# Inverse root of a recurrence's output norm: ScalarE logarithm and exponential in place of square root and VectorE reciprocal

## The chip, the cores and the metric

One core of a Trainium2 chip runs the whole program. The metric is the device time of one execution in microseconds (us). A core has five engines that run side by side, each through its own list of instructions, in the order of that list: TensorE (PE in the profile; its weight loads are PEld), VectorE (DVE), ScalarE (ACT), GpSimd (POOL) and SyncE (SP, which here only issues DMA transfers). They wait for one another by semaphores. ScalarE evaluates functions such as the square root from a table, and an instruction of its own (ACT_TABLE_LOAD in the profile) brings in another set of functions.

## The reference, cut to what matters

The reference runs two layers. Layer 0 is a recurrence over 32 mini-batches of 16 tokens for 4 sequences and 32 heads of 16 channels, beside a gated feed-forward layer; layer 1 is an attention with compressed keys and values beside an expert layer. All is float32. The change concerns the norm of the recurrence's output, which is taken over the 16 channels of each head:

```python
def _ln(x, gamma, beta):
    mu = x.mean(-1, keepdims=True)
    var = x.var(-1, keepdims=True)
    return gamma * ((x - mu) / jnp.sqrt(var + EPS)) + beta      # EPS = 1e-6, 16 channels
...
Z1_bar = xq @ W1_s - eta_mb * Attn1 @ grad + b1_bar
out = xq + _ln(Z1_bar, ln_w, ln_b)
...
out = ys.transpose(1, 0, 3, 2, 4).reshape(Bb, Ll, HS)
out = _ln(out, post_norm_weight, post_norm_bias)               # over 512 channels
return out @ o_w.T
```

## The kernel before, in words

**The first stage** (0 to about 1030 us) does layer 0. The 512 tokens of each sequence are cut into 8 chunks of 64; a chunk of all four sequences has 256 columns (CW), and four mini-batches. The outer loop runs over the 32 mini-batches. Each step (`weights_out`, `first_product`, `queries_out`, `gradient`, `out_operands`, `update`, `emit_out`) is a chain through all engines: products of the state with keys and queries into `pz` and `pso`, a norm and its gradient on VectorE with small ScalarE operations (L339 to L373), block-diagonal copies `g_bd` on VectorE and ScalarE (L378), `gh` on GpSimd (L404), the update of the state `wacc` on PE, and copies of the new state into `wq_bd` (L315) and `wh` (L318) for the next step.

**Filling work.** Between the parts of a step, `fill(us)` takes pieces of other work from a generator and gives PE something to do: `between(ch)` holds, for each chunk, the feed-forward layer (`gate_up`: 11 pairs of gate and up products `pf` into two PSUM buffers, a Silu `sg` on ScalarE, L458, and a product `hid` on VectorE, L459; `down`: products `pd`), the features of the next chunk (`norm_turn` transposes the normed input into `xT`, copied by ScalarE, L140; `keys`, `queries`, `token_tile`) and `finish(ch - 1)`, the norms of the chunk that the recurrence has just left. Each piece names a number of microseconds as its share. No chunk's steps begin before its features are done. `finish` is called 8 times, once for each chunk; I number the calls by it. Its first part is put after the ninth of the 11 gate pairs. For chunk 6 the pieces come at other places, and for chunk 7, where no feed-forward work is left, `finish` runs between the `latents` products. From all this the builder makes one list for each engine, and within the program's dependences it puts instructions of different pieces in another order than they are written.

**`finish(ch)`** works on `zb`, the chunk's centred output, 128 partitions by 4 blocks of 256 columns. ScalarE squares it (L524). Then twice, for two blocks at a time (128x512): PE sums each group of 16 partitions by a product with `bones` (L528, into a `pj` PSUM buffer, of which there are two for all uses); ScalarE takes the root of the mean plus epsilon into `rs` (named `pn_rs`, one buffer for both halves, L530); VectorE inverts it (L531) and multiplies `zb` by it (L532). ScalarE applies weight and bias in four operations (L534), GpSimd adds the queries (L537). The second norm follows: VectorE adds the four blocks up (L516, L517), PE multiplies by `onesd` for the mean (L540, `pj<-pn_sq,onesd` in the profile), VectorE subtracts it (L541), ScalarE squares (L542), VectorE adds up, PE sums (L548), ScalarE takes a root of 128x2 (L549), and PE multiplies by `wo` (L554). PE products go through the helper at L100, so they carry its line and are told apart by their tiles.

**The later stages** (from 1030 us) do the expert layer and the attention, and are bound by PE; nothing in them is touched.

Of the kernel before, what the change touches and what calls it, by code (L numbers as in the profile page):

```python
# [13 lines left out]
AF = mybir.ActivationFunctionType  # L14
# [9 lines left out]
NH, HD, K = 32, 16, 16  # L24
# [31 lines left out]
def trunk_kernel(ctx: ExitStack, tc: tile.TileContext, a: dict, out: bass.AP):  # L56
    nc = tc.nc
# [17 lines left out]
    eps_ttt = const.tile([P, 1], F32, tag="eps_ttt", name="eps_ttt")  # L75
# [13 lines left out]
    with ExitStack() as px:  # L89
# [9 lines left out]
        def mm(out, lhsT, rhs, start=True, stop=True):  # L99
            nc.tensor.matmul(out, lhsT=lhsT, rhs=rhs, start=start, stop=stop, skip_group_check=True)  # L100

        def psum():
            return ps_pj.tile([P, 512], F32, tag="pj", name="pj")
# [10 lines left out]
        def row_norm(dst, src, nm):  # L114
            st = wk.tile([P, 6], F32, tag="ln_st", name=f"ln_st{nm}")
            mv = wk.tile([P, 2], F32, tag="ln_mv", name=f"ln_mv{nm}")
            nc.vector.bn_stats(out=st, in_=src)
            nc.vector.bn_aggr(out=mv, in_=st)
            rs = wk.tile([P, 1], F32, tag="ln_rs", name=f"ln_rs{nm}")
            nc.scalar.activation(rs, mv[:, 1:2], AF.Sqrt, bias=eps_ln, scale=1.0)  # L120
            nc.vector.reciprocal(rs, rs)
            nc.vector.tensor_scalar(dst, src, mv[:, 0:1], rs, ALU.subtract, ALU.mult)

        def transposed(src):
            pt = psum().rearrange("p (c t) -> p c t", c=NC)
            for c in range(NC):
                nc.tensor.transpose(pt[:, c, :], src[:, c * P : (c + 1) * P], ident)
            return pt
# [385 lines left out]
        def over_blocks(t, z):  # L514

            nc.vector.tensor_add(t[:, :2], z[:, :2], z[:, 2:])  # L516
            nc.vector.tensor_add(t[:, 0], t[:, 0], t[:, 1])  # L517
            return t[:, 0]

        def finish(ch):  # L520
            store = nc.sync if ch + 1 < NCHUNK else nc.scalar
            zb = zbs.pop(ch)
            sq = wk.tile([P, NC, CW], F32, tag="pn_sq", name=f"pn_sq_{ch}", bufs=1)
            nc.scalar.activation(sq, zb, AF.Square)  # L524
            for j in range(2):
                half = zb[:, 2 * j : 2 * j + 2].rearrange("p c t -> p (c t)")
                pv = psum()
                mm(pv, bones, sq[:, 2 * j : 2 * j + 2].rearrange("p c t -> p (c t)"))  # L528
                rs = wk.tile([P, 512], F32, tag="pn_rs", name=f"pn_rs_{ch}_{j}", bufs=1)
                nc.scalar.activation(rs, pv, AF.Sqrt, bias=eps_ttt, scale=1.0 / HD)  # L530
                nc.vector.reciprocal(rs, rs)  # L531
                nc.vector.tensor_mul(half, half, rs)  # L532
            for be in range(NC):
                nc.scalar.activation(  # L534
                    zb[:, be], zb[:, be], AF.Identity, bias=beta_ch[:, be : be + 1], scale=gamma_ch[:, be : be + 1]
                )
            nc.gpsimd.tensor_add(zb, zb, q1[ch])  # L537
            yield 1.72
            pm = psum()[:, :CW]
            mm(pm, onesd, over_blocks(sq, zb))  # L540
            nc.vector.tensor_sub(zb, zb, pm.unsqueeze(1).to_broadcast([P, NC, CW]))  # L541
            nc.scalar.activation(sq, zb, AF.Square)  # L542
            over_blocks(sq, sq)
            yield 0.43
            pt = psum()
            rt = wk.tile([P, 2], F32, tag="pn_rt", name=f"pn_rt_{ch}")
            for u in range(2):
                mm(pt[:, u : u + 1], sq[:, 0, u * P : (u + 1) * P], onesd[:, :1])  # L548
            nc.scalar.activation(rt, pt[:, :2], AF.Sqrt, bias=eps_ttt, scale=1.0)  # L549
            nc.vector.reciprocal(rt, rt)  # L550
            for u in range(2):
                po = psum()
                for be in range(NC):
                    mm(po, zb[:, be, u * P : (u + 1) * P], wo[:, be, :], be == 0, be == NC - 1)  # L554
                t = yf.pop((ch, u))
                nc.vector.scalar_tensor_tensor(t, po, rt[:, u : u + 1], t, ALU.mult, ALU.add)
                for b2 in range(2):
                    store.dma_start(
                        out=yd[2 * u + b2, ch * CT : (ch + 1) * CT, :], in_=t[b2 * CT : (b2 + 1) * CT, :]
                    )  # L560

                xt = wk.tile([P, HS], F32, tag="xt", name=f"x1_{ch}_{u}", bufs=4)
                row_norm(xt, t, f"1_{ch}_{u}")
                xns[ch, u] = xt
                yield 4.4
            if ch >= NCHUNK - 2:
                t = wk.tile([P, NC, CW], F32, tag="xT", name=f"xl_{ch}", bufs=3)
                part = parts[ch] = t.rearrange("p c w -> p (c w)").rearrange("p (u c e x) -> p u c e x", u=2, c=NC, e=E)
            for u in range(2):
                if ch >= NCHUNK - 2:  # L570
                    xs = part[:, u]
                else:
                    xs = wk.tile([P, NC, E, 32], F32, tag="xs", name=f"xs_{ch}_{u}")
                nc.scalar.copy(xs, transposed(xns.pop((ch, u))).rearrange("p c (j e) -> p c e j", e=E))
                store.dma_start(out=xe_d[2 * ch + u], in_=xs)
                yield 0.6
# [50 lines left out]
        def between(ch):  # L627

            fin = finish(ch - 1) if ch > 0 else iter(())
            if ch + 1 == NCHUNK:  # L630
                latent_operands()
# [120 lines left out]
        for n in range(NM):  # L752
# [12 lines left out]
            if n + 1 < NM:  # L765
                while (n + 1) // CH not in done:
                    fill(1.0)
                pre = prepare(n + 1)
        fin = finish(NCHUNK - 1)
        for us in LAST_FINISH:  # L770
            fill(us)
# [15 lines left out]
    scale = 1.0 / math.sqrt(D)  # L787
# [493 lines left out]
```

## Time and profile before

| | us |
|---|---|
| median of three runs | 2126.29 (2125.87 to 2128.31) |
| the profiled execution | 2126.91 |
| its span, first to last instruction | 2125.1 |
| PE busy | 2041.5 |
| DVE busy | 1199.9 |
| ACT busy | 860.5 |
| POOL busy | 504.4 |
| all ACT_TABLE_LOAD instructions, 87 | 111.6 |
| granted PE clock, mean | 0.988 of full speed |

The 111.6 us are 87 times 1283 ns. A line of the profile that names a group gives line, engine, operation, output and inputs with their shapes, the count, then busy time in us and the mean ns of one, then the idle time of the engine just before them and what ended it. A line of the waits gives who waited for whom, the total, the number of times and the longest. A line of the timeline gives start, duration, engine, line, operation and count, and in brackets the idle time before it. PE's busy time is modelled, since matmuls overlap; a busy PE is one that has work, not one at its peak.

### The profile page before, as it was taken

What the parts mean: (1) busy time and instruction counts of PE and PEld (TensorE: products, weight loads), DVE (VectorE), ACT (ScalarE), POOL (GpSimd) and SP (SyncE); (2) the same over time, 40 slices, a digit from 0 to 9 for tenths busy, and PEclk for the clock granted to TensorE, in tenths of its full rate; (3) what the DMA queues carried; (4) which work ended last, traced back from release to release, by engine and by line L of the source; (5) the groups of instructions that cost most, each with busy time, mean ns of one, the idle gap of its engine ahead of it and who ended that gap; (6) DMA issues with size and microseconds to landing.
All of it is one profiled execution on the core that took longest, in us unless ns stands there. A gap on an engine that the chain in (4) does not pass through costs nothing.

```text
span 2125.1 us, 29355 instructions
## 1 busy us (share of the span) xinstructions
PE 2041.5 (96%) x9932; PEld 1169.6 (55%) x9932; DVE 1199.9 (56%) x2452; ACT 860.5 (40%) x1733; POOL 504.4 (24%) x555
## 2 busy tenths in 40 slices
PE   8999999999999998997899999999999999999999
PEld 6777777767676765744344344444444444444444
DVE  5445656565737475633111485766666665766663
ACT  2334343434334343312001364555545554555552
POOL 5233333323333332302000121111111111142110
PEclk9999999999999999999999999999999999999999
DMA  6546464645454646445831143443334333433332
GB/s 187 161 133 185 120 190 116 193 114 174 138 165 127 183 120 200 116 123 178 300 98 29 29 99 79 93 98 79 78 81 106 78 80 73 101 78 76 91 96 75
DMA packets 336496, 257.19 MB, mean 121 GB/s; under 512 B 107099, under 2 KB 264988, under 8 KB 335324
## 3 DMA queue, kind: packets, MB, share of 16 engines
q1 hardware_dynamic: 322320, 243.89, 42.8%
q10 hardware_dynamic: 11500, 5.32, 0.9%
q0 software_dynamic: 2528, 6.12, 0.8%
q8 instruction: 80, 1.31, 0.3%
q14 instruction: 68, 0.56, 0.1%
HBM read 159.50 MB, written 29.62 MB: 89 GB/s over the span
## 4 chain that ended last, share of the span: by engine, by line
PE 78%; DVE 6%; SPq 6%; DMA 4%; ACT 3%; issue 2%; POOL 1%; ACTq 0%; DVEq 0%; POOLq 0%
PE pj L100 14%; PE pf L100 11%; PE po L1119 9%; PE pc L1106 8%; PE sc L1038 8%; PE pq L1028 7%; PE pd L100 5%; SPq L1098 4%; PE epo L957 3%; PE epu L906 2%; PE pso L100 2%; PE pk L1020 2%; PE epg L906 2%; PE pz L100 2%; SPq L845 1%
## 5 line engine op out<-in xcount | busy, mean ns | idle before, releaser
L1013 POOL TENSOR_TENSOR kT<-t_k,t_k 32x512 f32<-32x512 f32 x64 | 80.7, 1260 | 802.6 <-PE pq L1028 339.9
L1043 ACT ACTIVATE prob<-sc,mx 128x512 f32<-128x512 f32 x256 | 174.3, 683 | 198.9 <-DVE mx L1040 194.1
L1038 PE MATMUL sc<-kT,qT 96*128 96x512 f32 x512 | 230.9, 593 | 1.7 <-ACT prob L1043 1.4
L1119 PE MATMUL po<-vo,ctxT 128*128 128x512 f32 x512 | 230.0, 592 | 0.7 <-ACT ctxT L1108 0.7
L1106 PE MATMUL pc<-prT,lv 128*128 128x512 f32 x496 | 224.8, 596 | 3.2 <-DVE t_q L1003 3.2
L1067 DVE STREAM_TRANSPOSE tt<-prob 128x512 f32<-128x512 f32 x252 | 173.0, 706 | 56.2 <-ACT prob L1048 48.5
L1028 PE MATMUL pq<-cq,uq 128*128 128x512 f32 x384 | 178.0, 600 | 7.3 <-ACT ctxT L1108 7.3
L100 PE MATMUL pf<-xT,wg 128*128 128x256 f32 x704 | 173.5, 389 | 8.2 <-DVE hid L459 7.1
L1048 ACT ACTIVATE prob<-prob,sm 128x512 f32<-128x512 f32 x256 | 176.4, 713 | 0.0
L1040 DVE TENSOR_REDUCE mx<-sc 128x1 f32<-128x512 f32 x256 | 168.2, 678 | 5.8 <-PE sc L1038 3.8
L100 PE MATMUL pf<-xT,wu 128*128 128x256 f32 x704 | 167.5, 381 | 0.0
L1038 PEld LDWEIGHTS sc<-kT,qT 96*128 96x128 f32 x512 | 96.9, 190 | 126.1 <-issue 120.1
L100 PE MATMUL pd<-wd,hid 128*128 128x512 f32 x352 | 164.7, 600 | 1.4 <-DMA wd<-in_wd 1.4
L1119 PEld LDWEIGHTS po<-vo,ctxT 128*128 128x128 f32 x512 | 96.9, 190 | 123.4 <-issue 117.9
L1106 PEld LDWEIGHTS pc<-prT,lv 128*128 128x128 f32 x496 | 94.7, 191 | 123.2 <-issue 118.4
L100 PEld LDWEIGHTS pf<-xT,wg 128*128 128x128 f32 x704 | 132.1, 192 | 34.9 <-DVE hid L459 10.1
L100 PEld LDWEIGHTS pf<-xT,wu 128*128 128x128 f32 x704 | 134.4, 191 | 18.9 <-DMA wu<-in_wu 0.4
L1028 PEld LDWEIGHTS pq<-cq,uq 128*128 128x128 f32 x384 | 73.6, 192 | 101.9 <-issue 90.5
L459 DVE SCALAR_TENSOR_TENSOR hid<-pf,us,sg 128x256 f32<-128x256 f32 x88 | 41.9, 478 | 139.1 <-ACT sg L458 138.4
L297 POOL TENSOR_SCALAR sk<-k,m 128x256 f32<-128x256 f32 x64 | 60.1, 950 | 182.4 <-PE pz L100 173.7
L1003 DVE SCALAR_TENSOR_TENSOR t_k<-pk,b_UK,trig_k 32x512 f32<-32x512 f32 x64 | 47.9, 748 | 90.4 <-ACT kT L1021 89.8
L100 PEld LDWEIGHTS pd<-wd,hid 128*128 128x128 f32 x352 | 63.8, 190 | 61.8 <-issue 48.6
(247 smaller groups left out, 3065.0 us busy)
## 6 DMA issues: line engine op xcount, KB each, us to landing
prT<-tt SPq DMA_DIRECT2D x1008, 64.0 KB, 2.0
wd<-in_wd SPq DMA_DIRECT2D x176, 256.0 KB, 3.0
wg<-in_wg SPq DMA_DIRECT2D x88, 256.0 KB, 2.9
wu<-in_wu SPq DMA_DIRECT2D x88, 256.0 KB, 3.4
rows<-rows SPq DMA_DIRECT2D x128, 66.0 KB, 2.2
kv<-rows SPq DMA_DIRECT2D x32, 264.0 KB, 4.5
gu<-in_gu SPq DMA_DIRECT2D x3, 2048.0 KB, 7.8
xt<-in_x SPq DMA_DIRECT2D x32, 128.0 KB, 3.3
```

Source lines behind the costliest of these rows:

```text
L100: nc.tensor.matmul(out, lhsT=lhsT, rhs=rhs, start=start, stop=stop, skip_group_check=True)
L906: nc.tensor.matmul(ps, lhsT=w[:, c, col : col + P], rhs=xe[:, :, c, e, :], start=(c == 0), stop=(c == NC - 1))
L1013: nc.gpsimd.tensor_sub(t[RD:mid, :], t1[RD:mid, :], t2[RD:mid, :])
L1028: nc.tensor.matmul(pq, lhsT=w[f"uq{i}"][:, h, :], rhs=cq[:, i, b, :], start=(i == 0), stop=(i == nq - 1))
L1038: pin(nc.tensor.matmul(ps, lhsT=qT[:KQ, i * P : (i + 1) * P], rhs=kT[:KQ, :], start=True, stop=True))
L1040: pin(nc.vector.tensor_reduce(mx, ps, AX.X, ALU.max, negate=True))
L1043: pin(nc.scalar.activation(pr, ps, AF.Exp, bias=mx, scale=1.0, accum_out=sm))
L1048: pin(nc.scalar.mul(pr, pr, sm))
L1067: nc.vector.transpose(out=tt[:, :, :, i, :], in_=pr.rearrange("p (kb e j) -> p kb e j", e=2, j=K))
L1098: nc.sync.dma_start(out=prT[32 * kq : 32 * kq + 32, :, qb, :], in_=src[32 * qb : 32 * qb + 32, :, kq, :])
L1106: pin(nc.tensor.matmul(pc, lhsT=lv[:, b, k, :], rhs=prT[:, k, :], start=(k == 0), stop=(k == E - 1)))
L1119: nc.tensor.matmul(po[e], lhsT=ctxT[:, h, e * P : (e + 1) * P], rhs=w["vo"][:, h, :], start=(h == 0), stop=(h == HPG - 1),)
```

## The change

In `finish`, the root by ScalarE and the inverse by VectorE become a logarithm and an exponential, both by ScalarE: 1/sqrt(v) = exp(-0.5 ln v). The product with `zb` stays, and so do all buffers. The other roots of the kernel (L120, L347, L549) keep their form. The lines behind the change move by one.

```diff
                 rs = wk.tile([P, 512], F32, tag="pn_rs", name=f"pn_rs_{ch}_{j}", bufs=1)
-                nc.scalar.activation(rs, pv, AF.Sqrt, bias=eps_ttt, scale=1.0 / HD)
-                nc.vector.reciprocal(rs, rs)
+
+                nc.scalar.activation(rs, pv, AF.Ln, bias=eps_ttt, scale=1.0 / HD)
+                nc.scalar.activation(rs, rs, AF.Exp, scale=-0.5)
                 nc.vector.tensor_mul(half, half, rs)
```

## The prediction

> **What bounds the kernel now.** I read the page's busy times first, then the two norm lines in the groups, then the waits of PE up to 1050 us (the recurrence lies there, the eight calls of `finish` between 187 and 985 us), and then the timeline of each call, because what counts is who waits at that place.
>
> ```profile
> PE 2041.5 (96%) x9932; PEld 1169.6 (55%) x9932; DVE 1199.9 (56%) x2452; ACT 860.5 (40%) x1733; POOL 504.4 (24%) x555
> ```
>
> PE is the bound, and every engine runs a list that was fixed at build time. So an instruction costs time only where it makes PE wait, and PE waits wherever its next instruction is not ready, even if later ones are. The groups that the change touches, with two neighbours that give prices:
>
> ```profile
> L1048 ACT ACTIVATE prob<-prob,sm 128x512 f32<-128x512 f32 x256 | 176.4, 713 | 0.0
> ...
> L530 ACT ACT_TABLE_LOAD x13 | 16.7, 1283 | 0.2
> ...
> L530 ACT ACTIVATE pn_rs<-pj,eps_ttt 128x512 f32<-128x512 f32 x16 | 11.0, 688 | 10.7 <-DVE zb L532 8.4 <-PE pj L100 2.2
> ```
>
> ```profile
> L531 DVE RECIPROCAL pn_rs<-pn_rs 128x512 f32<-128x512 f32 x16 | 53.6, 3350 | 19.8 <-ACT pn_rs L530 19.8
> ...
> L532 DVE TENSOR_TENSOR zb<-zb,pn_rs 128x512 f32<-128x512 f32 x16 | 11.0, 688 | 0.1
> ```
>
> The reciprocal is the longest single operation of VectorE here, and a ScalarE table load costs nearly two activations. Where PE waits:
>
> ```profile
> PE wacc L100 <- DVE g_bd L378: 11.5, 3, 9.3
> ...
> PE pj L100 <- DVE pn_sq L517: 3.3, 4, 1.7
> PE pso L100 <- POOL gh L404: 3.0, 3, 1.3
> ```
>
> The 9.3 us is one wait, in the call for chunk 6 (I write F0 to F7 for the eight calls). The 3.3 us are waits of the mean's product (L540) for the end of the norm chain (L517). In the windows around F0 to F7 (209 us together) PE is busy 186.9 us: **22 us** is all that the change could win back there. F6 in the timeline:
>
> ```profile
> 832.48 1.28 ACT L530 ACT_TABLE_LOAD   x1
> ...
> 833.77 0.69 ACT L530 ACTIVATE pn_rs<-pj,eps_ttt 128x512 f32<-128x512 f32 x1
> ...
> 834.49 3.35 DVE L531 RECIPROCAL pn_rs<-pn_rs 128x512 f32<-128x512 f32 x1 [2.46 <-ACT pn_rs L530]
> ...
> 839.38 3.35 DVE L531 RECIPROCAL pn_rs<-pn_rs 128x512 f32<-128x512 f32 x1 [0.81 <-ACT pn_rs L530]
> ...
> 844.90 2.50 POOL L537 TENSOR_TENSOR zb<-zb,q 128x1024 f32<-128x1024 f32 x1 [12.96 <-ACT zb L534]
> ...
> 850.71 1.08 PE L100 MATMUL wacc<-g_bd,km 128*32 128x64 f32 x32 [9.31 <-DVE g_bd L378]
> ```
>
> Both reciprocals stand ahead of the gradient's last operations in VectorE's list, so PE, which ran dry at 841.4, gets `g_bd` only at 850.7.
>
> **Counts.** Removed: 16 reciprocals, 53.6 us of VectorE. Sixteen square roots become sixteen Ln of the same operands (I take 0.69 us, the row's price). Added: 16 Exp from SBUF; the nearest rows are 0.68 (an Exp from PSUM, L1043) and 0.71 (a scaled copy from SBUF, L1048); I take 0.71, and an error of 0.1 us in all 32 would be 3 us at most. Table loads, counted in the built order of instructions: one stands before every Ln and every Exp (32, with two different set numbers, where the square roots had 13), the Silu line has 30 for 34, the second root 4 for 1: 105 for 87, or 18 x 1.283 = 23.1 us. ScalarE gets 23.1 + 11.4 = **34.5 us more**, and all of it in the eight places. Over 180 to 980 us ScalarE is busy 306 of 800 us, so the total has cover; the place decides.
>
> **The chain, alone.** From the first load to the data of the mean's product. Before: load 1.28, then twice (root 0.69, reciprocal 3.35, product 0.69), Identity x2 1.09, POOL addition 2.35, two additions 0.69 + 0.43 = **15.3 us**. After: load 1.28, Ln 0.69, load 1.28, Exp 0.71, product 0.69, and then, since there is one `pn_rs` buffer and the built order puts the next load behind the wait for that product, again load 1.28, Ln 0.69, Identity 0.54, load 1.28, Exp 0.71; in F0 to F3 and F5 an Identity 0.54, a Silu load 1.28 and a Silu 0.47 come ahead of the last two Identities (1.09), and the same 3.47 follow: **16.0 us**. Without the Silu (F6, F7; the product 0.69 counts instead) 14.4. So 53.6 us of reciprocals leave, and the chain of each call hardly changes: the loads take their place.
>
> **What moves.** The builder orders by its own estimate, and in the built order the mean's product comes sooner on PE: ahead of L540 there are 14.3, 17.8, 17.5, 17.5, 19.3 and 16.7 us of PE work after the group-sum products in F0 to F5 (before: 20.6, 21.2, 19.7, 21.4, 20.6, 19.9), and in F6 none at all (before: the whole of ten gate products). These are my sums of row prices (a gate pair 3.45, a 512-wide product 0.86, and so on). A chain no shorter, and a PE that comes for it sooner, is a wait.
>
> F6, walked with the rows: Ln done at 834.46, Exp 836.45, product 837.2, second Ln 839.2, Exp 841.75, product 842.5, Identities 843.4, POOL 845.8, additions 847.0. PE stands from 834.3 to 847.0 (12.7 us), then the mean's product, gate pairs 2 and 3 (6.9, and some 1.7 more, since the first group after the long wait now takes 3.57 instead of 1.89 us), and `wacc` at about 856; `g_bd` is ready by 853.6 then. Before, both pairs were done and `wacc` began at 850.7 after its wait; the next pair began at 853.0, now at 856.5, with the mean's product (0.5) already behind it: **+3.0**.
>
> The others the same way, by when PE has done an equal amount: F0 **+4.5** (the ScalarE copies of `wq_bd` and Silu 9, 10 queue behind the loads: `pz` waits 2.7 us, then the mean's product 2.4); F1 **+1.0** (1.6 us for the mean's product, partly given back); F2 **+3.5** (the chunk's transposed input, L140, and the mean's subtraction, L541, come late, and the next chunk's keys wait for both); F3 **+2.5** (the same two); F4 **-1.3** (the waits 1.6 for `g_bd` and 1.3 for `gh` shrink: VectorE is free earlier); F5 **+0.9** (1.6 for `wacc`, 2.1 for the mean); F7 **-1.0** (same PE order, latent products released a little earlier). Sum **+13.1**. Later waits of PE that hang on DMA (3.0 us of idle time in 480 to 500, 3.1 in 600 to 620) will swallow some; I take 2 off: **+11**. The profiled execution took 2126.9 (span 2125.1), the median of the three runs is 2126.3; from the median, **2137**.
>
> **A rule against the row.** In the rows above the load starts 0.02 us after the activation ahead of it (831.41 + 1.05) and the root 0.01 us after the load; all 87 loads take 1283 ns and no more. The Trainium skill ("ScalarE: Activation LUTs", section "What ACT_TABLE_LOAD costs") gives the same 1283 ns, and a drain of some 1380 ns beside it, 2.66 us for a switch. By that each call's chain would be about 5 x 1.38 = 6.9 us longer and the sum some 50 us higher, an estimate from that page which no gap in this trace supports. The same page (section "Table sets: the hidden batching unit") says that a logarithm and then an exponential need one load, from a set that holds both. That would take 2.6 us off each chain and turn the forecast to about no change; the built order has two, so I go by the order.
>
> **Rivals.** (a) *Faster, 2118.* VectorE's release decides: with 53.6 us gone there, the gradients come sooner, and of the 22 us of PE idle time some 8 go. For it: the 9.3 us wait, F4. Against: PE's list puts the mean's product ahead of `wacc` in F6. It decides once the chain is under some 13 us, that is if a load is hidden under the product or the additions. (b) *Same, 2126.* The added waits are swallowed downstream, since PE waits again on DMA (`kv`, `wd`) in every chunk and the recurrence's own chain is shorter without reciprocals. Against: after F0, F1, F4 such idle time is under 1.5 us per 20 us. (c) *Much slower, 2150.* The waits on PE also delay the recurrence step under way and drop the granted clock (0.74 in 840 to 860 after the 9.3 us wait), costing 1.7 us or more a call in addition: 13 + 8 x 1.4 = 24. (d) *One load serves each pair* though two are listed: 16 x 1.28 = 20 us less ScalarE work, 5 us of it on PE's waits: 2121.
>
> **Numbers.** Forecast 0.57, (a) 0.11, (b) 0.17, (c) 0.12, (d) 0.03. The ends without any cover are -22 and +34.5 us; the cases do not reach them. Leaving out (a) and the upper part of (c): **2121 to 2149**. A measurement of this kernel can tell about 0.2% (4.3 us) from no change: faster (a) and half of (d), 0.12; within, (b), the other half of (d) and the forecast's lower edge, 0.21; slower 0.67.
>
> **What would show it.** 32 loads on the two new lines at 1283 ns with nothing between load and activation; Ln and Exp near 0.69; the second Ln's load starting after the first product; in F6 a wait of PE for L517 near 12 us in place of 9.3 for `g_bd`; waits for L517 of 1 to 2.5 us in F0 to F5, and together some 20 us for the 3.3 now. I am wrong if PE finds the mean ready in F0 to F3, if F6's wait is under 9 us, or if the loads run while ScalarE waits.

## The result and the profile after

The changed kernel takes 2138.7 us (median of four runs, 2136.8 to 2141.1) where the kernel before, beside it, took 2126.1: a ratio of 1.0058, interval 1.0042 to 1.0074, or 12.6 us more. The forecast was 2137. A second comparison (experiment 5) gave 1.0069 [1.0051, 1.0087]. The profiled execution took 2141.1 us, its span was 2139.3.

The page of the changed kernel, busy times:

```profile
PE 2038.5 (95%) x9932; PEld 1168.9 (55%) x9932; DVE 1142.4 (53%) x2436; ACT 894.1 (42%) x1767; POOL 503.5 (24%) x555
```

VectorE lost 57.5 us, ScalarE gained 33.6, PE has the same work and stands 100.8 us (span less busy time) instead of 83.6. The groups of the changed lines (one line down from before):

```profile
L531 ACT ACT_TABLE_LOAD x16 | 20.5, 1283 | 4.2 <-DVE zb L533 4.0
L532 ACT ACT_TABLE_LOAD x16 | 20.5, 1283 | 0.3
...
L531 ACT ACTIVATE pn_rs<-pj,eps_ttt 128x512 f32<-128x512 f32 x16 | 11.0, 688 | 1.0 <-PE pj L100 0.9
...
L532 ACT ACTIVATE pn_rs<-pn_rs 128x512 f32<-128x512 f32 x16 | 10.1, 630 | 0.2
...
L533 DVE TENSOR_TENSOR zb<-zb,pn_rs 128x512 f32<-128x512 f32 x16 | 11.1, 691 | 58.7 <-ACT pn_rs L532 58.7
```

Every activation has a load of its own. VectorE, freed of 53.6 us of reciprocals, now stands 58.7 us ahead of the product with `zb`: it waits where it used to work. PE's waits up to 1060 us:

```profile
PE pj L100 <- DVE pn_sq L517: 20.2, 6, 12.8
...
PE pj L100 <- DVE zb L542: 5.2, 2, 2.6
...
PE pz L100 <- ACT wq_bd L315: 3.5, 3, 2.3
PE pj L100 <- ACT xT L140: 3.3, 4, 1.5
PE wacc L100 <- DVE g_bd L378: 2.1, 2, 1.4
```

The waits for the norm's end (L517) went from 3.3 to 20.2 us; those for `g_bd` fell from 11.5 to 2.1. F6 in the timeline, PE and then ScalarE:

```profile
843.16 1.98 PE L100 MATMUL pj<-pn_sq,bones 128*128 128x512 f32 x4 [1.51 <-ACT pn_sq L524]
858.00 1.19 PE L100 MATMUL pj<-pn_sq,onesd 128*128 128x256 f32 x2 [12.85 <-DVE pn_sq L517]
...
868.28 0.65 PE L100 MATMUL wacc<-g_bd,km 128*32 128x64 f32 x32
```

```profile
844.42 0.69 ACT L531 ACTIVATE pn_rs<-pj,eps_ttt 128x512 f32<-128x512 f32 x1
845.13 1.28 ACT L532 ACT_TABLE_LOAD   x1
846.42 0.63 ACT L532 ACTIVATE pn_rs<-pn_rs 128x512 f32<-128x512 f32 x1
847.85 1.28 ACT L531 ACT_TABLE_LOAD   x1 [0.80 <-DVE zb L533]
```

PE has nothing between the group sums and the mean, and stands for the whole chain. The last line shows the load itself behind the wait for the first product.

### The profile page after: what moved, and what is told of

It is laid out like the page before. It is cut to its first block, busy times and chain, and to the rows that moved or that the text cites. A ratio compares the mean times of both kernels' runs of the same rounds, so it can differ in the third digit from the quotient of the medians.

```text
span 2139.3 us, 29357 instructions
## 1 busy us (share of the span) xinstructions
PE 2038.5 (95%) x9932; PEld 1168.9 (55%) x9932; DVE 1142.4 (53%) x2436; ACT 894.1 (42%) x1767; POOL 503.5 (24%) x555
## 4 chain that ended last, share of the span: by engine, by line
PE 74%; SPq 7%; DMA 5%; ACT 5%; DVE 5%; issue 2%; POOL 1%; ACTq 0%; DVEq 0%; POOLq 0%
PE pj L100 13%; PE pf L100 11%; PE po L1120 8%; PE pc L1107 8%; PE sc L1039 8%; PE pq L1029 6%; PE pd L100 6%; SPq L1099 5%; PE epo L958 3%; PE epu L907 2%; PE epg L907 2%; PE pso L100 2%; PE pk L1021 2%; SPq L846 2%; PE pz L100 2%
## 5 line engine op out<-in xcount | busy, mean ns | idle before, releaser
L404 POOL TENSOR_SCALAR gh<-grad,m 128x256 f32<-128x256 f32 x64 | 62.9, 993 | 140.3 <-DVE grad L373 139.9
```

## The experiments

The theory at the start: the table loads stand on the norm's chain, PE's list comes for the chain's end too soon, and the meeting of the two is the loss. Rivals: PE's order alone would cost the same with any content; the second ScalarE operation costs; each load beyond the 87 of before costs 12.6 / 18 = 0.70 us wherever it stands ("rival 3"). Experiments 1 to 4, 5 to 8, 9 to 11 and 12 were measured as four groups, each beside its own runs of the kernel before; the ratios and their 95% intervals are to these. "Lag" is how much later than before an instruction starts in the profiled execution.

**1. Two activations, no loads between them.**

```diff
-                nc.scalar.activation(rs, pv, AF.Ln, bias=eps_ttt, scale=1.0 / HD)
-                nc.scalar.activation(rs, rs, AF.Exp, scale=-0.5)
+                nc.scalar.activation(rs, pv, AF.Sqrt, bias=eps_ttt, scale=1.0 / HD)
+                nc.scalar.activation(rs, rs, AF.Identity, scale=-0.5)
```

> The changed kernel with the logarithm replaced by the square root and the exponential by an Identity with the same scale (the inverse is left out, so zb is multiplied by the wrong factor; sizes, buffers and the number of operations stay). The built order has the mean's product as early as in the changed kernel (11.5, 15.1, 14.8, 14.8, 14.6, 14.6, 0 us of PE work ahead of it in F0 to F6 by the same prices; changed kernel: 11.5, 15.1, 14.8, 14.8, 17.1, 14.6, 0), but 77 table loads in all, 7 of them on the norm's line, instead of 105 with 32. My theory (the loads on the norm's chain make PE wait): without them the chain is 2 x (0.69 + 0.63 + 0.69) + 1.09 + 2.35 + 1.1 + at most one load, about 9.5 us, the waits for L517 in F0 to F5 go and F6 waits about 7.5 instead of 12.85; so 2120, between 2116 and 2125, faster than before. Rival 1 (PE's order alone: the mean's product came forward, and that would cost the same with any content): 2134 to 2139, with waits for L517 near 20 us. Rival 2 (the second ScalarE operation itself, not the loads): 2131 or more.

Measured: 0.9943 [0.9923, 0.9963], 12 us under before and below my range. The sign was mine, the gain twice mine. PE's waits:

```profile
PE pj L100 <- DVE pn_sq L517: 9.6, 2, 8.9
...
PE wacc L100 <- DVE g_bd L378: 0.9, 2, 0.6
```

Only F6 keeps a long wait (8.9; I expected 7.5). PE's order up to the expert stage is the changed kernel's but for some products `pd` in F4. So neither the early order nor the second activation (624 ns here) costs by itself.

**2. Half the loads.**

```diff
+            rs = wk.tile([P, 2, 512], F32, tag="pn_rs", name=f"pn_rs_{ch}", bufs=1)
             for j in range(2):
-                half = zb[:, 2 * j : 2 * j + 2].rearrange("p c t -> p (c t)")
                 pv = psum()
                 mm(pv, bones, sq[:, 2 * j : 2 * j + 2].rearrange("p c t -> p (c t)"))
-                rs = wk.tile([P, 512], F32, tag="pn_rs", name=f"pn_rs_{ch}_{j}", bufs=1)
-
-                nc.scalar.activation(rs, pv, AF.Ln, bias=eps_ttt, scale=1.0 / HD)
-                nc.scalar.activation(rs, rs, AF.Exp, scale=-0.5)
-                nc.vector.tensor_mul(half, half, rs)
+                nc.scalar.activation(rs[:, j], pv, AF.Ln, bias=eps_ttt, scale=1.0 / HD)
+            for j in range(2):
+                half = zb[:, 2 * j : 2 * j + 2].rearrange("p c t -> p (c t)")
+                nc.scalar.activation(rs[:, j], rs[:, j], AF.Exp, scale=-0.5)
+                nc.vector.tensor_mul(half, half, rs[:, j])
```

> The changed kernel with one pn_rs buffer of two halves: both logarithms first, then both exponentials. Same operations and result; 89 table loads instead of 105, 17 instead of 32 on the two lines. PE's order as in the changed kernel (11.1, 15.1, 14.8, 14.8, 14.6, 14.6, 0 us ahead of the mean's product). My theory: the chain loses two loads and the wait of the second logarithm for the first product, 16.0 - 2.6 - 0.7 = 12.7 us; F0 about +2, F1 to F5 within 0.5 of before, F4 -1.5, F6 +0.5 (its wait near 9.5 us): 2126, between 2122 and 2130. Rival 1 (order alone): 2134 to 2139. Rival 3 (a load costs its time wherever it stands, so in proportion to the number: 12.6 / 18 = 0.70 us for each load beyond the 87): 2 more than before, +1.4, 2127.5: the total does not tell this from my theory, the waits do: by rival 3 they fall evenly, by mine F6 keeps 9 us or more and the rest falls under 3 us.

Measured: 0.9973 [0.9962, 0.9985], faster than before by 5.7 us, outside my range. The waits are as my theory had them: 11.6 us for L517, of which 9.4 in F6 and 2.2 in F4.

```profile
PE pj L100 <- DVE pn_sq L517: 11.6, 2, 9.4
```

What I had not counted: F0 adds no lag where I had put 2 us, and F7 is 7.0 us shorter in this profile; how much of that can be put down to the edit is in the last section.

**3. F6's mean behind the gate pairs.** On the changed kernel. In F6 alone the builder is told to keep the product for the mean at the place where the program writes it (the helper `mm` returns its instruction for this):

```diff
-            mm(pm, onesd, over_blocks(sq, zb))
+            t = mm(pm, onesd, over_blocks(sq, zb))
+            if ch == 6:
+                tc.keep_in_program_order(t)
```

> The changed kernel with all its 105 loads; only the mean's product of F6 is put back behind gate pairs 2 and 3 on PE (38 us of work ahead of it instead of none; F0 to F5 as in the changed kernel). My theory (the wait is where the chain meets PE's order): the 12.85 us wait goes; but VectorE's list still has the gradient's last operations behind L517, so PE does the two gate pairs and then waits for g_bd, some 9 to 10 us, as before; F6 then costs +0.3 instead of +3.75: 2135, between 2133.5 and 2136.5. Rival (loads cost their time wherever PE stands): 2138 to 2139.5, unchanged. Rival (PE's order is the whole of F6): g_bd comes at once behind the pairs and F6 gains 9: 2126 to 2130.

Measured: 1.0050 [1.0030, 1.0070]; the time does not tell it from the changed kernel. The trace does: the 12.85 us became 10.2 us for `g_bd`, and F6 adds 1.25 us of lag instead of 3.76 (I expected 0.3).

```profile
PE wacc L100 <- ACT g_bd L378: 11.2, 2, 10.2
```

PE's order is not the whole of F6: VectorE's list has the gradient behind L517 too.

**4. The mean later in all calls.** Also on the changed kernel, with its 32 loads on the norm's lines.

```diff
             yield 1.72
+            if ch < 6:
+                yield 0.0
             pm = psum()[:, :CW]
-            mm(pm, onesd, over_blocks(sq, zb))
+            tc.keep_in_program_order(mm(pm, onesd, over_blocks(sq, zb)))
```

> The changed kernel with the loads kept (107), and the mean's product and what follows it put later in all calls but the last: one more turn of the filling work stands ahead of it (20.5, 22.8, 22.8, 23.9, 23.9, 23.9, 38.0 us of PE work in F0 to F6, 13.7 in F7 as before). Other PE work moves forward with it, so the order is not otherwise the same. My theory: the waits for L517 (20.2 us) go, those for L542 (5.2) may stay or move to the product with wo; F0 keeps its wait for wq_bd (2.3, ScalarE's queue); F6 as in the kernel with its mean behind the gates. So 2129, between 2125 and 2133. Rival 3 (a load costs 0.70 us wherever it stands): 2138 to 2140. Rival (the lateness only moves: what needs the mean's subtraction waits instead): 2136 or more.

Measured: 1.0027 [1.0013, 1.0041]: half of the loss is gone. No wait for L517 is left, but in F6 VectorE's list has the gradient behind L517 as in the changed kernel: `wacc` waits 14.4 us for `g_bd` (10.5 in F6), and 7.4 us go to L140. The lists of the other engines moved too, not PE's alone.

```profile
PE wacc L100 <- ACT g_bd L378: 14.4, 4, 10.5
PE pj L100 <- ACT xT L140: 7.4, 6, 2.0
```

**5. The changed kernel again.**

> The changed kernel as it is, as the measure for the others of this call: by its first comparison 1.0058 of before, between 1.004 and 1.0075.

Measured: 1.0069 [1.0051, 1.0087].

**6. The change in F6 alone.**

```diff
+                if ch == 6:
                     nc.scalar.activation(rs, pv, AF.Ln, bias=eps_ttt, scale=1.0 / HD)
                     nc.scalar.activation(rs, rs, AF.Exp, scale=-0.5)
+                else:
+                    nc.scalar.activation(rs, pv, AF.Sqrt, bias=eps_ttt, scale=1.0 / HD)
+                    nc.vector.reciprocal(rs, rs)
```

> Before, with logarithm and exponential in F6 alone; F0 to F5 and F7 keep root and reciprocal, and their PE order is that of before (17.9, 18.5, 16.9, 18.6, 18.4, 17.2, 0, 13.7 us of PE work ahead of the mean's product). 90 table loads instead of 87. My theory (each call costs what its own wait costs): the lag behind before is 0 up to F6 and +3.75 us from there (a wait for L517 of 12.8 in place of 9.3 for g_bd): ratio 1.0016, 1.0005 to 1.0025. Rival 3 (0.70 us for each load beyond the 87): +2.1, 1.0010, which the time does not tell apart from it; the trace does, by whether the lag sets in at that wait. Rival (the F6 wait is an inheritance of the earlier calls' delay): no lag, 1.0000.

Measured: 1.0010 [1.0000, 1.0021]. In the profile the lag is 2.36 at F6's group sums (1.85 of it was there at F0's) and 5.75 at F7's: F6 alone costs 3.4 us, beginning at a wait of 12.85 us for L517. Over F7 the lag fell back to 1.8; the last section says why I read no gain into that.

**7. Half the loads, and F6's mean behind the gates** (edits 2 and 3 together).

> Both logarithms first and then both exponentials, as in the second experiment, and the mean's product of F6 behind gate pairs 2 and 3. My theory: the wait of 9.4 us for L517 turns into one for g_bd of about 6 to 7 (VectorE's list keeps the gradient's last operations behind L517, and the chain is 2.6 to 3.4 us shorter than in the changed kernel), and what PE does in between is no longer late: F6 gains 2 to 4 against before where the second experiment gained 1.3 to 2 there. Ratio 0.996, between 0.9945 and 0.998 (the second experiment had 0.9973). Rival (order of the mean's product does not matter once the loads are halved): 0.9973.

Measured: 0.9950 [0.9933, 0.9968], with experiment 10 the fastest version that computes the reference, 2112.8 us against 2123.9. F6 gives 3.9 us of lag back.

**8. Before, with the mean later** (edit 4 on the kernel before).

> Before, with root and reciprocal kept, and the mean's product put later by the same edit as in the fourth experiment (20.5, 22.8, 22.8, 23.9, 23.9, 23.9, 38.0, 13.7 us of PE work ahead; 89 loads). It tells whether the fourth kernel's 1.0027 is the loads or its order. My theory: the loads that stay in the fourth kernel cost there by wq_bd (ScalarE's queue) and g_bd; without them the late order is no loss: 0.9975 to 1.0005. Rival (the late order itself costs the 0.27%): 1.002 to 1.004.

Measured: 0.9996 [0.9986, 1.0006]. The late place of the mean is neutral by itself.

**9. Root, then exponential.**

```diff
-                nc.scalar.activation(rs, pv, AF.Ln, bias=eps_ttt, scale=1.0 / HD)
+                nc.scalar.activation(rs, pv, AF.Sqrt, bias=eps_ttt, scale=1.0 / HD)
                 nc.scalar.activation(rs, rs, AF.Exp, scale=-0.5)
```

> The changed kernel with the logarithm replaced by the square root, the exponential kept (the result is no inverse root: exp(-0.5 sqrt(v)) in its place). 107 table loads, 31 on the two lines, where the changed kernel has 105 and 32: the same loads. But the built order puts the mean's product later: 16.2, 18.5, 16.9, 16.5, 17.1, 16.3, 38.0, 13.7 us of PE work ahead of it in F0 to F7 (changed: 11.5, 15.1, 14.8, 14.8, 17.1, 14.6, 0, 13.7; before: 17.9, 18.5, 16.9, 18.6, 18.4, 17.2, 38.0, 13.7). My theory (it takes both: a chain with loads, and a PE order that comes for it too soon): the waits for L517 fall from 20.2 to under 4 us, F6 waits about 10 us for g_bd as in the third experiment; what stays is ScalarE's queue (wq_bd, 2.3 in F0): ratio 1.002, between 1.0005 and 1.004. Rival 3 (each load beyond the 87 costs 0.70 us wherever it stands): 20 loads, +14 us, 1.0066.

Measured: 0.9968 [0.9956, 0.9980]. I expected a small loss; it is 6.8 us faster than before, with 107 loads. That ends rival 3, and it ends the part of my theory that had the kernel lose something to the loads even in a fitting order. Its waits:

```profile
PE wacc L100 <- DVE g_bd L378: 7.8, 3, 6.7
...
PE pj L100 <- DVE pn_sq L517: 2.0, 3, 0.9
...
PE pz L100 <- ACT wq_bd L315: 1.8, 2, 1.1
```

F6 of this kernel, VectorE: parts of the gradient (L350 to L363) stand in the gap in which ScalarE loads, between the norm's two products, and the rest up to the gradient itself (L373) ahead of L516. In the changed kernel all of these stood behind L517; its two lines at the place follow those of this kernel.

```profile
834.11 0.69 DVE L533 TENSOR_TENSOR zb<-zb,pn_rs 128x512 f32<-128x512 f32 x1 [4.41 <-ACT pn_rs L532]
834.72 0.17 DVE L350 TENSOR_TENSOR rl<-r,kv 128x16 f32<-128x16 f32 x1
834.81 0.42 DVE L362 TENSOR_TENSOR pair<-pair,kv 128x256 f32<-128x256 f32 x1
835.26 0.42 DVE L363 TENSOR_TENSOR pair<-pair,xh 128x256 f32<-128x256 f32 x1
839.33 0.69 DVE L533 TENSOR_TENSOR zb<-zb,pn_rs 128x512 f32<-128x512 f32 x1 [3.65 <-ACT pn_rs L532]
```

```profile
857.35 0.50 DVE L517 TENSOR_TENSOR pn_sq<-pn_sq 128x256 f32<-128x256 f32 x1
857.77 0.16 DVE L350 TENSOR_TENSOR rl<-r,kv 128x16 f32<-128x16 f32 x1
```

**10. Half the loads, F6's mean behind the gates, and the gradient ahead of the additions.** As 7, and in F6 alone the first addition for the mean is kept in its place in the same way:

```diff
-        def over_blocks(t, z):
+        def over_blocks(t, z, hold=False):
...
-            nc.vector.tensor_add(t[:, :2], z[:, :2], z[:, 2:])
+            t0 = nc.vector.tensor_add(t[:, :2], z[:, :2], z[:, 2:])
+            if hold:
+                tc.keep_in_program_order(t0)
...
-            mm(pm, onesd, over_blocks(sq, zb))
+            t = mm(pm, onesd, over_blocks(sq, zb, ch == 6))
```

> As the seventh kernel (both logarithms, then both exponentials; F6's mean behind the gate pairs), and in F6 VectorE's two additions for the mean (L516, L517) stand behind the gradient's operations in its list, so that these wait only for the second product of the norm and no longer for GpSimd's addition. My theory: g_bd comes sooner by the 2.4 us of GpSimd's addition and the 1.1 to 1.2 us of the two additions: the wait of 6.8 us becomes 3 to 4.5 (4.5 or more if the gradient's operations are stretched while GpSimd adds, as one was in the profile before: 2.56 us for 0.42), and the time is 2.5 to 3.5 us under the seventh kernel's of this call. Rival: the gradient's chain itself decides, the wait stays at 6 to 7 and the time with it.

**11. The seventh kernel again.**

> The seventh kernel again, as the measure for the tenth in this call: 0.995 of before, between 0.993 and 0.997.

Measured: 0.9951 [0.9933, 0.9969] for the tenth kernel and 0.9957 [0.9945, 0.9970] for the seventh again, not told apart; I had expected the tenth to be 2.5 to 3.5 us faster. The wait shrank as expected, from 6.75 to 3.86 us, and `wacc` began 12.74 us after the group sums instead of 15.64. At the next `wacc` only 1.1 of those 2.9 us are left (37.58 against 38.72 us in the seventh kernel). The timeline of the tenth kernel shows where they went:

```profile
841.92 1.08 PE L100 MATMUL wacc<-g_bd,km 128*32 128x64 f32 x32 [3.86 <-DVE g_bd L378]
843.52 1.14 PE L100 MATMUL pso<-a_bd,gh 128*32 128x68 f32 x32 [0.51 <-POOL gh L404]
844.58 3.78 PE L100 MATMUL pf<-xT,wg 128*128 128x256 f32 x8
848.16 2.04 PE L100 MATMUL pf<-xT,wu 128*128 128x256 f32 x8
```

0.51 us is a new wait for `gh`, and the gate pair took 3.78 + 2.04 where it took 2.50 + 1.89 in the seventh kernel.

**12. Logarithm, then sigmoid**, one function changed against the changed kernel:

```diff
-                nc.scalar.activation(rs, rs, AF.Exp, scale=-0.5)
+                nc.scalar.activation(rs, rs, AF.Sigmoid, scale=-0.5)
```

> The changed kernel with the exponential replaced by the sigmoid (the result is 1/(1 + sqrt(v)), no inverse root); the logarithm is the changed kernel's. 109 table loads, 16 and 16 of them on the two lines as in the changed kernel, but the built order is that of the ninth kernel but for one 128x512 product of F4 and two others (16.2, 18.5, 16.9, 16.5, 18.0, 16.3, 38.0, 13.7 us of PE work ahead of the mean's product). So only the pair of logarithm and exponential gets the early order, though both pairs run with two loads. My theory (an order laid out as if there were no load between the two): the time is the ninth kernel's, 0.997 of before, between 0.9955 and 0.9995, the waits for L517 stay under 3 us. Rival (the logarithm or its own load is what costs, and the ninth kernel was fast because it had the root): 1.003 or more, with waits for L517 of 5 us or more.

Measured: 0.9968 [0.9952, 0.9984]. The groups and the waits of this kernel:

```profile
L531 ACT ACT_TABLE_LOAD x16 | 20.5, 1283 | 1.9 <-DVE zb L533 0.8 <-DVE rl L350 0.8
L532 ACT ACT_TABLE_LOAD x16 | 20.5, 1283 | 0.3
...
L531 ACT ACTIVATE pn_rs<-pj,eps_ttt 128x512 f32<-128x512 f32 x16 | 11.0, 687 | 0.2
...
L532 ACT ACTIVATE pn_rs<-pn_rs 128x512 f32<-128x512 f32 x16 | 10.1, 630 | 0.2
```

```profile
PE wacc L100 <- DVE g_bd L378: 7.7, 3, 6.7
...
PE pj L100 <- DVE pn_sq L517: 2.2, 3, 0.9
```

The same four groups as in the changed kernel, to the last 0.1 us, and some 19 us less time (0.9968 beside 1.0058 of 2124 us). What differs is the order in the lists (and four more loads on other lines).

| kernel | loads on the norm's lines | order of the lists | ratio to before |
|---|---|---|---|
| changed (and again, 5) | 32 | early mean | 1.0058, 1.0069 |
| 1, root and Identity | 7 | early mean | 0.9943 |
| 2, half the loads | 17 | early mean | 0.9973 |
| 4, changed, mean written later | 32 | latest mean, F6's gradient behind L517 | 1.0027 |
| 9, root and exponential | 31 | late mean, F6's gradient ahead of L516 | 0.9968 |
| 12, logarithm and sigmoid | 32 | late mean, F6's gradient ahead of L516 | 0.9968 |

So the loss needs both: 32 loads, and an order that has no room for them. The place of the mean's product is not the whole of that order, as experiment 4 shows: with it later still, F6 waits 10.5 us for `g_bd`, where experiments 9 and 12 wait 6.7. No run put the logarithm and exponential themselves into the order of experiments 9 and 12, and neither of these two computes the reference. The builder gave room when the pair was root and exponential or logarithm and sigmoid, and none when it was logarithm and exponential, although each pair ran with two loads. That it counted one load or none for the pair is what I infer from this; no run shows its estimate. The Trainium skill ("ScalarE: Activation LUTs", section "Table sets: the hidden batching unit") says that a logarithm followed by an exponential takes one load, since one set holds both; here 16 and 16 loads ran.

## Why the prediction was right, and where its sizes were off

The profiled executions, call by call: how much each adds to the lag, from its group sums to the next call's (F7: to the first instruction of the expert stage that follows a wait), against the one profile of before. Up to F5 the lists of experiment 3 are those of the changed kernel, so its profile is a third execution of F0 to F5.

| us | F0 | F1 | F2 | F3 | F4 | F5 | F6 | F7 | sum |
|---|---|---|---|---|---|---|---|---|---|
| predicted | +4.5 | +1.0 | +3.5 | +2.5 | -1.3 | +0.9 | +3.0 | -1.0 | +13.1 |
| changed | +6.3 | +1.7 | +2.2 | +0.7 | -1.5 | +0.7 | +3.8 | -1.2 | +12.8 |
| changed again | +4.9 | +1.4 | +1.3 | +2.1 | -1.5 | +0.7 | +4.0 | -3.1 | +9.8 |
| experiment 3 | +7.4 | +2.0 | +5.1 | +3.4 | -1.1 | +0.7 | | | |

One program's executions differ by 2.5 us in F0, 3.9 in F2, 2.7 in F3 and 1.9 in F7, so what these add is known no better than that. F1, F4, F5 and F6 repeat within 0.6 us.

**Counts and prices.** The 32 loads, 105 in all, nothing between load and activation: as said. Ln 688 ns; the exponential took 630 instead of the 710 I took, 1.3 us over 16, on a row of another line.

**The chain and its place.** "A chain no shorter, and a PE that comes for it sooner, is a wait" is what happened: 20.2 us for L517 where I had put some 20. F6 waited 12.85 for my 12.7, F0 2.34 and 2.30 for my 2.7 and 2.4. The waits for L517 in F1 and F5 were in my range of 1 to 2.5 us (1.73, 2.16), those in F2 and F4 under it (0.44, 0.78), and in F3 PE found the mean ready, which I had named as a sign of being wrong: there it had just stood 1.47 us for L140. Experiments 1 and 12 each take one half of that sentence away; the waits for L517 fall to 9.6 us (8.9 of it in F6) and to 2.2, and each time the kernel is faster than before. I took the order from the built list without asking what it was laid out for; had I asked, another order would have been among the rivals.

The PE work that I put ahead of the mean was too large, in both kernels alike. In F0 I had 20.6 us before and 14.3 after; from the first group sum to the mean's product, without waits, the profiles have 18.33 (204.79 - 186.21 - 0.25) and 12.26 (203.57 - 186.67 - 4.64); the expectations above have 17.9 and 11.5. The argument rests on the difference, 6.3, and that came as 6.1.

**F0 was too small, by 0.4, 1.8 and 2.9 us in the three executions.** The waits were right; the clock was not in the sum. Windows over F0, before and then changed:

```profile
200.00:206.00 6.00, 5.75 (x75) 3.84 (x75) 3.08 (x8) 2.82 (x5) 5.06 (x5) 1.00 0.58 174
206.00:212.00 6.00, 5.76 (x24) 3.70 (x23) 5.56 (x14) 2.31 (x6) 1.14 (x3) 1.00 0.25 83
```

```profile
200.00:206.00 6.00, 3.06 (x18) 2.37 (x19) 3.16 (x6) 2.73 (x7) 2.25 (x1) 0.62 0.00 0
206.00:212.00 6.00, 6.00 (x67) 4.74 (x66) 3.56 (x10) 1.88 (x4) 2.79 (x5) 0.81 0.00 1
```

The value behind the five engines' busy times is the granted clock: over two waits of 2.3 us within 5 us and the work behind them it is 0.62 and 0.81. The four profiles whose F0 has that first wait of 2.34 us for `wq_bd` (changed, changed again, 3 and 4) have a mean clock of 0.97 to 0.99 over F0, the other ten 1.00. All of F0 has 2.0 us more PE busy time for the same 913 instructions (108.84 against 106.83), and 1.0 in the second profile. This is rival (c)'s mechanism, but in the first profile in F0 only: F1 to F5 had a mean clock of 1.00 (before: 1.00, and 0.99 in F3), and F6 0.94 where it had 0.95, so its price of 1.4 a call did not come.

**F2 and F3** were too large by 3.1 and 2.6 us together in the two profiles of the changed kernel, and too small by 2.5 in experiment 3's, where the clock was 0.97 in both calls. The waits that I named came: for L542 (L541 before) 2.63 and 2.57 us, for L140 0.49 and 1.47. What differs is PE's busy time: against before it was 0.8 and 2.0 us less in the first profile, and 2.7 and 1.0 us more in experiment 3's. So no miss of mine is shown here beyond what executions differ by.

**The 2 us that I took off for later waits** were not absorbed where I had put them: in the first profile, after F2 the wait for `hid` went from 2.41 to 2.22 us and the one ahead of it grew from 0.60 to 0.99, after F3 it stayed at 3.12. Only the first of the two hangs on DMA, as I had read both (VectorE stands 3.44 us for `kv` there). The second hangs on the recurrence itself: `hid` waits for a Silu that stands behind the copies of `g_bd` in ScalarE's list, so it moves along with the lag.

**The total.** That +11 stands so close to +12.6 is luck in part: F0 and F6 too small, 2 us taken off that did not go, and terms for F2, F3 and F7 of which a profile shows no more than the sign or the rough size.

**F6** came 0.8 to 1.0 larger than my walk, with the wait as walked: the pair behind `wacc` began 26.2 us after the group sums (869.34 - 843.16) for my 24.0, since the gate pairs took 9.3 us at the low clock for my 8.6, the mean's product and the step from `wacc` to that pair 2.0 for my 0.9, and the wait ended 0.3 later. The pair's first product then ran at 1.99 us where before it took 3.57, and gave most of the difference back; I had left that out.

**Rivals.** (a) named 2118 and said that it would need a chain under 13 us; experiments 9 and 12, which do not compute the reference, reach 2117 to 2118 with two loads in each half of the chain, by an order that fits it. (b) had too much faith in later idle time. (d) is out: 32 loads ran. Its 2121 and the "about no change" above it are two prices for the same case, one load for each pair, and no run tests either.

## What to carry to other kernels

Before pricing a change that swaps functions or engines, compare the built order of every list with that of before: an operation that the builder takes for cheaper than it is moves its consumers forward, and on the bound engine that can become a wait (12.85 us in F6 here). Time of an engine off the bound (34 us more on ScalarE here) is neither a cost nor free: with 32 loads on the norm's lines the kernel took 12.6 us more than before in one order, and 6.8 less in another. Grouping what shares a table set (both logarithms, then both exponentials) halves the loads for the price of a larger buffer, and with one consumer moved it made a loss of 0.6 to 0.7% a gain of 0.4 to 0.5%.

## What the hardware showed that I had not expected

**The granted clock of one stretch swings between executions.** F7 before, and in the second experiment, from the group sums to the expert stage's first wait, which holds the same 194 PE instructions:

```profile
949.03:1032.67 83.64, 73.00 (x194) 38.02 (x194) 23.33 (x49) 15.36 (x40) 10.76 (x17) 0.90 0.60 211
```

```profile
946.96:1023.60 76.64, 68.94 (x194) 36.51 (x194) 16.91 (x47) 20.45 (x45) 10.75 (x17) 0.96 0.63 224
```

7.0 us less: 2.9 of idle time, and 4.1 of busy time at a granted clock of 0.96 instead of 0.90. The busy part cannot be put down to the edit. Experiment 6 has F7 with root and reciprocal as before, and the same 194 instructions took as little:

```profile
954.78:1035.51 80.73, 68.93 (x194) 36.01 (x194) 23.34 (x49) 15.32 (x40) 10.77 (x17) 0.96 0.65 227
```

The changed kernel's two profiles have 72.05 us at 0.92 and 69.51 at 0.96. What the second, seventh, tenth and eleventh kernels share is less idle time in F7, 7.5 to 8.6 us where the other ten profiles have 8.7 to 11.9, and so the shortest F7 of all (76.6 to 78.5 us). Why the clock differs between executions is open.

**VectorE stands while GpSimd adds.** In the tenth kernel a 128x256 VectorE operation that takes 0.42 us elsewhere took 2.57, and ended 0.28 us after GpSimd's addition (836.81 + 2.61 = 839.42):

```profile
837.13 2.57 DVE L370 TENSOR_TENSOR xh<-xh,s 128x256 f32<-128x256 f32 x1
```

```profile
836.81 2.61 POOL L540 TENSOR_TENSOR zb<-zb,q 128x1024 f32<-128x1024 f32 x1 [10.31 <-DVE s L365]
```

The kernel before had the same, beside the addition at 844.90, and so had the ninth, beside its addition at 841.24; both again ended 0.28 us after it:

```profile
845.12 2.56 DVE L370 TENSOR_TENSOR xh<-xh,s 128x256 f32<-128x256 f32 x1
```

```profile
841.45 2.44 DVE L371 SCALAR_TENSOR_TENSOR u<-xh,u 128x256 f32<-128x256 f32 x1
```

So work that is moved beside GpSimd's addition on VectorE gains less than its place says. The Trainium skill ("SBUF — State Buffer", section "SBUF: two separate sides") has a rule for it: an operation of VectorE with two SBUF inputs and one of GpSimd that reads SBUF exclude each other for a whole instruction. These three cases agree with it.
